# Two half-width matmul tiles, and seven products for eight, in the third layer of a four-layer graph kernel

## The chip, the cores and the metric

The kernel runs on one core of one Trainium2 chip. The metric is the device time of one execution in microseconds (us). Before the change it is 2273.68 us, the median of three runs (2272.29 to 2274.11).

## What is computed

There are 32 independent graphs (batches) of 512 nodes with 128 features, each with a dense weighted 512 x 512 adjacency matrix, everything in fp32. Four graph layers follow each other; each normalizes its input, applies a graph network and adds the result to its input. What matters here is the third of them ("stage three"), which is itself a network of four sublayers over the same adjacency matrix:

```python
def _layer(nodes, adj, ws, bs, wd, bd, wn, bn, wu, bu):
    src = nodes @ ws + bs
    src_agg = jnp.einsum('bjv,bij->biv', src, _l2norm(adj, 2))
    dst = nodes @ wd + bd
    dst_agg = jnp.einsum('bjv,bji->biv', dst, _l2norm(adj, 1))
    self_rep = nodes @ wn + bn
    upd = jnp.concatenate([src_agg, self_rep, dst_agg], axis=2)
    return jnp.tanh(upd @ wu + bu)
...
for i in range(NUM_LAYERS):
    if i < half:
        stashed.append(fpass)
    elif i == half:
        fpass = jnp.concatenate([fpass, stashed[NUM_LAYERS - i - 1]], axis=2)
    else:
        fpass = jnp.concatenate([fpass, stashed[NUM_LAYERS - i], stashed[NUM_LAYERS - i - 1]], axis=2)
    fpass = _layer(fpass, adj, *params[i])
```

So each sublayer multiplies projected features with the matrix (aggregation over the rows) and with its transpose, and adds a term of the node itself. Sublayers 2 and 3 also take `f1`, the output of sublayer 0, and sublayer 3 takes `f0`, the input of all.

## The kernel before

All work of a batch is listed as operations of an engine with an estimated time, what they read and what they write (`Plan.op`). `Plan.order` then plays all 32 batches through at once: on each engine the ready operation with the earliest due time goes first (due times lie `PERIOD` = 37 us a batch apart), and an operation waits in the plan until its buffers are free. The result is a fixed instruction order for each engine, with several batches interleaved on TensorE (PE). The buffers are places in a few pools: `s2` (a 128 x 512 tile, 36 of them), `s4` (twice as much, 5), `s8` (a whole matrix, 10) and 8 PSUM banks. Where the plan leaves PE idle for more than 0.7 us, `kept_warm` puts in products of the identity (`ps_idle`).

In stage three, `w_sb` holds weights into which the update matrix `wu` has been multiplied at the start, so that aggregation, node term and update fall together. Per batch:

- `a` and `aT`, the matrix and its transpose as four chunks of 128 x 512, are scaled in place by the inverse norms (L1096, DVE).
- Sublayers 0 and 2 (loop at L1107): `paired_rows` makes `sd`, both projections with bias (4 matmuls of 256 columns, L791 adds the bias); a node term of 512 columns and eight aggregation matmuls of 512 columns go into one PSUM bank (`ps_agg`), and tanh on ScalarE (ACT) ends the sublayer.
- Sublayer 1 with `fifteen` (L871 and on): eight aggregation matmuls of the turned features `f1r`, then 15 products of 256 columns, which give the terms of `f1` and of its two aggregates in sublayers 1, 2 and 3 at once (nine matrix products of two halves each would be 18). The sums before and after them are on DVE (L908).
- Sublayer 3 with `seven`: its projections of two inputs as seven products for eight, 14 matmuls of 128 columns, with DVE sums (L813); then two node terms and eight aggregation matmuls.

`mm` (L353) emits nearly all matmuls, `product` those of `fifteen` (L914), of `seven` (L835) and of the last layer's gates (L516). The stationary operand has 128 columns in all of them. `at_ends` (the first two batches and the last) turns matrices by PE transposes (`ps_t`, L733, L753, L876); the others turn them by DMA. GpSimd (POOL) does the negative half powers of the normalizations (L688, L1077) and nothing wide.

## Time and profile before

| | |
|---|---|
| median of three runs | 2273.68 us |
| the profiled execution's own time | 2275.95 us |
| its span | 2274.2 us |
| matmul operations, in two records each but for transposes, which have one | 3844 |
| DVE busy, mean step of a 128x512 operation | 1607.0 us, 687 ns |
| GpSimd's powers of 128x4 and 128x8 | 1186 ns and 1857 ns |

The span is from the first to the last instruction of the program; the execution's own time lies 1.75 us above it. "Busy" is time in which an engine had any instruction under way. For PE the lengths of matmuls overlap, so the pace is read from one start to the next.

### The profile page before, as it was taken

Reading aid. Unit: us, or ns where it says so; the run is one execution under the profiler, and the core shown is the slowest. Engines: PE = TensorE matmul, PEld = TensorE weight load, DVE = VectorE, ACT = ScalarE, POOL = GpSimd, SP = SyncE. Lnnn points to the kernel's source line nnn. Section 1 sums busy time; section 2 is a strip of 40 time slices with the busy share of each in tenths; the row PEclk is TensorE's granted clock in tenths of the full one; section 3 lists DMA queues with packets and bytes.
Section 4 is the critical chain, followed back from the end, with each engine's and each line's share of the span. In section 5 each row is a group of like instructions: output and inputs, shape, how many; then the busy total and the mean of one; then the engine's idle time right before and its main releaser. Section 6 shows DMA issues by size and latency. Waiting matters only on the chain.

```text
span 2274.2 us, 25755 instructions
## 1 busy us (share of the span) xinstructions
PE 2263.3 (100%) x7608; PEld 1311.8 (58%) x7608; DVE 1607.0 (71%) x4346; ACT 1101.4 (48%) x2563; POOL 216.6 (10%) x203
## 2 busy tenths in 40 slices
PE   9999999999999999999999999999999999999999
PEld 6555565555565555555555655555555556555556
DVE  6756676767777777767777777777677777776655
ACT  7643554544445544455544455445555444552422
POOL 2100100100100100001001001000010010010000
PEclk9999999999999999999999999999999999999999
DMA  8032333444333443334443334443344333333212
GB/s 295 29 105 77 111 99 117 139 128 127 119 105 121 130 130 120 107 117 135 132 123 121 104 120 130 130 120 108 115 136 134 122 117 106 121 99 91 79 42 65
DMA packets 199052, 263.03 MB, mean 116 GB/s; under 512 B 25984, under 2 KB 130688, under 8 KB 198912
## 3 DMA queue, kind: packets, MB, share of 16 engines
q1 hardware_dynamic: 198624, 261.26, 37.6%
q8 instruction: 60, 0.98, 0.2%
q14 instruction: 80, 0.66, 0.1%
q10 hardware_dynamic: 288, 0.13, 0.0%
HBM read 199.18 MB, written 62.13 MB: 115 GB/s over the span
## 4 chain that ended last, share of the span: by engine, by line
PE 95%; DMA 2%; DVE 2%; ACT 0%; issue 0%; SPq 0%; POOL 0%; ACTq 0%; DVEq 0%; POOLq 0%
PE ps_agg L353 61%; PE ps_fifteen L914 9%; PE ps_sd L353 7%; PE ps_seven L835 4%; PE ps_seven L516 4%; PE ps_upd L353 3%; PE ps_gate L353 3%; PE ps_lin L353 1%; PE ps_msg L353 1%; PE ps_node L353 1%; DMA last<-turn_last 0%; DMA turned<-turn_turned 0%; DMA bounce<-invT 0%; DMA r_sb<-in_brow 0%; DMA turn_turned<-blk 0%; DMA rows<-bounce 0%
## 5 line engine op out<-in xcount | busy, mean ns | idle before, releaser
L353 PE MATMUL ps_agg<-a,sd 128*128 128x512 f32 x768 | 385.3, 593 | 0.0
L353 PE MATMUL ps_agg<-aT,sd 128*128 128x512 f32 x768 | 380.5, 593 | 0.4 <-DVE sd L791 0.2
L688 POOL TENSOR_TENSOR sc<-v,neg_half 128x4 f32<-128x4 f32 (+1 forms) x127 | 150.6, 1186 | 1710.5 <-DVE v L649 1603.5
L353 PEld LDWEIGHTS ps_agg<-aT,sd 128*128 128x128 f32 x768 | 136.6, 191 | 86.4 <-issue 77.5
L700 ACT ACTIVATE h<-xr,nb,sc 128x128 f32<-128x128 f32 x384 | 157.9, 482 | 49.1 <-DVE nb L696 49.1
L353 PEld LDWEIGHTS ps_agg<-a,sd 128*128 128x128 f32 x768 | 137.0, 191 | 62.0 <-issue 53.8
L353 PE MATMUL ps_sd<-w_sb,f 128*128 128x256 f32 x512 | 145.6, 380 | 0.9 <-ACT f L1112 0.9
L353 PEld LDWEIGHTS ps_sd<-w_sb,f 128*128 128x128 f32 x512 | 94.4, 190 | 77.6 <-issue 61.7
L1136 ACT ACTIVATE f<-c,cf_sb 128x512 f32<-128x512 f32 x64 | 46.2, 722 | 179.8 <-DVE c L1135 179.8
L353 PE MATMUL ps_agg<-f,w_sb 128*128 128x512 f32 x256 | 130.9, 593 | 0.1
L353 PE MATMUL ps_agg<-aT,f1r 128*128 128x512 f32 x256 | 130.7, 592 | 0.0
L353 PE MATMUL ps_agg<-a,f1r 128*128 128x512 f32 x256 | 130.7, 592 | 0.0
L353 PE MATMUL ps_agg<-aT,h 128*128 128x512 f32 (+2 forms) x260 | 128.7, 583 | 0.6 <-ACT h L673 0.6
L353 PE MATMUL ps_agg<-a,rep 128*128 128x512 f32 x256 | 125.5, 592 | 0.0
L353 PE MATMUL ps_agg<-aT,rep 128*128 128x512 f32 x256 | 121.6, 595 | 2.0 <-DVE rep L1049 1.8
L353 PE MATMUL ps_agg<-aT,msg 128*128 128x512 f32 (+1 forms) x264 | 116.7, 579 | 0.0
L791 DVE TENSOR_TENSOR sd<-ps_sd,rf_sb 128x512 f32<-128x512 f32 x128 | 87.9, 687 | 32.3 <-PE ps_sd L353 31.9
L1096 DVE TENSOR_TENSOR a<-a,rows 128x512 f32<-128x512 f32 x128 | 87.2, 687 | 16.7 <-PE ps_agg L353 16.1
L709 DVE STREAM_TRANSPOSE blk<-h 128x512 f32<-128x512 f32 x87 | 61.4, 706 | 51.4 <-ACT h L700 51.2
L1077 POOL TENSOR_TENSOR inv<-stat,neg_half 128x8 f32<-128x8 f32 x32 | 59.4, 1857 | 308.8 <-DVE stat L1076 287.9
L1096 DVE TENSOR_TENSOR aT<-aT,rows 128x512 f32<-128x512 f32 x128 | 86.4, 684 | 2.0 <-PE ps_agg L353 1.9
L1136 ACT ACTIVATE f<-ps_agg,cf_sb 128x512 f32<-128x512 f32 x32 | 22.0, 687 | 131.8 <-PE ps_agg L353 131.8
(229 smaller groups left out, 4424.6 us busy)
## 6 DMA issues: line engine op xcount, KB each, us to landing
aT<-in_adjt SPq DMA_DIRECT2D x124, 512.0 KB, 3.9
turn_turned<-blk SPq DMA_DIRECT2D x696, 64.0 KB, 1.8
turned<-turn_turned SPq DMA_DIRECT2D x174, 256.0 KB, 2.7
a<-in_adj SPq DMA_DIRECT2D x62, 512.0 KB, 7.5
rows<-bounce SPq DMA_DIRECT2D x32, 512.0 KB, 3.7
shares<-bounce SPq DMA_DIRECT2D x32, 512.0 KB, 4.4
x<-in_x SPq DMA_DIRECT2D x32, 256.0 KB, 2.7
out<-xr SPq DMA_DIRECT2D x31, 256.0 KB, 3.1
```

Source lines behind the costliest of these rows:

```text
L353: op("PE", t_mm(n), lambda: nc.tensor.matmul(out_of(ps.ap()), lhs(), rhs(), start=start, stop=stop), reads, [ps], later=later)
L516: op("PE", t_mm(H), lambda: nc.tensor.matmul(o[0](), weight(), data[0](), start=first, stop=True, skip_group_check=True), [data[1], wbuf], ...
L688: op("POOL", t_pow(n), lambda: nc.gpsimd.tensor_tensor(inv.ap()[:, :n], v8.ap()[:, :n], neg_half[:, :n], op=ALU.pow), [v8, NH], [(inv, {0})])
L700: op("ACT", t_act(D, 2), lambda c=c: nc.scalar.activation(h.ap()[:, c, :], xin.ap()[:, c, :], AF.Relu, bias=nb.ap()[:, c:c + 1], scale=inv ...
L709: op("DVE", t_tt(N), lambda: nc.vector.transpose(blk.ap().rearrange("p b (c r) -> p c b r", c=NC), m.ap().rearrange("p c (b s) -> p c b s" ...
L791: op("DVE", t_tt(N), lambda ps=ps, h=h: nc.vector.tensor_add(sd.ap()[:, 2 * h:2 * h + 2, :], ps.ap().rearrange("p (j v) -> p j v", j=2), a ...
L835: op("PE", t_mm(D), lambda j=j: nc.tensor.matmul(ps.ap()[:, k * H + j * D:k * H + (j + 1) * D], lhs()[:, j * P:(j + 1) * P], rhs(), start= ...
L914: op("PE", t_mm(H), lambda: nc.tensor.matmul(o[0](), weight(), data[0](), start=first, stop=True, skip_group_check=True), [data[1], wbuf], ...
L1077: roots = op("POOL", t_pow(2 * NC) + 0.4, lambda: nc.gpsimd.tensor_tensor(inv.ap()[:, :2 * NC], stat.ap(), neg_half, op=ALU.pow), [stat, N ...
L1096: op("DVE", t_tt(N), lambda m=m, c=c, s=s: nc.vector.tensor_mul(m.ap()[:, c, :], m.ap()[:, c, :], rows.ap()[:, s, :]), [(m, {c}), rows], [ ...
L1136: end = op("ACT", t_act(N, 1), lambda to=to, i=i, f_new=f_new: nc.scalar.activation(f_new.ap(), to.ap(), AF.Tanh, bias=cf_sb[:, i:i + 1]), ...
```

## The change

- Every matmul is now two: `by_halves` takes columns 0 to 63 and 64 to 127 of the stationary operand, one after the other, into the lower and upper 64 partitions of the output. This holds for the idle products too. PE transposes become such products with the identity (`turn_on_pe`).
- The aggregations of all four sublayers take seven products for eight: the matrix is seen as 2 x 2 blocks (even and odd chunk of a pair, left and right half of the columns), the features likewise (even and odd chunk, lower and upper 64). `made_of` prepares three combinations of blocks for each of `a` and `aT` on GpSimd (and replaces one block in place); `left_sums` makes four for the features on DVE. `side_by_side` emits two products with different operands, one for each half of the array.
- `features` replaces the node term, the aggregation and tanh of sublayers 0, 2 and 3. `lo` and `hi` list the products of the two halves in order; the sums of the seven products lie on DVE and one copy on ACT; tanh is taken in three parts.
- `fifteen` goes. `edges` makes the two aggregates of `f1` by the seven products, `second` adds the three terms of sublayer 1 as plain products, and the same three sources are node terms of `features` in sublayers 2 and 3.
- `seven` goes: `paired_rows` projects both inputs of sublayer 3 (8 matmuls of 256 columns).
- The pools become `s2` 29, `s4` 6, `s6` 4 (the combinations), `s8` 8; `PERIOD` becomes 41 us.

```diff
--- before.py
+++ after.py
@@ -22,17 +22,17 @@
 LN_EPS = 1e-5
 NORM_EPS = 1e-12
 L2_CHUNKS = (1, 1, 2, 3)
-PERIOD = 37.0
+PERIOD = 41.0
 ENDING = -3.5
...
-GATES = 5 * D
-FIFTEEN = GATES + 4 * D
-T_COLS = FIFTEEN + 6 * D
-LAYER_OF = (2, 3, 1)
+GATES = 0
+NODE = GATES + 4 * D
+T_COLS = NODE + 10 * (D // 2)
+HALVES = slice(0, P // 2), slice(P // 2, P)
...
@@ -296,7 +296,7 @@
-    plan = Plan(sb, psum, {"bank": 8, "s2": 36, "s4": 5, "s8": 10}, {"bank": 0, "s2": 4, "s4": 0, "s8": 0})
+    plan = Plan(sb, psum, {"bank": 8, "s2": 29, "s4": 6, "s6": 4, "s8": 8}, {"bank": 0, "s2": 3, "s4": 0, "s6": 0, "s8": 0})
...
@@ -349,21 +349,25 @@
+    def by_halves(to, weight, data, start, stop):
+        for c in HALVES:
+            nc.tensor.matmul(to[c], weight[:, c], data, start=start, stop=stop, skip_group_check=True)
+
     def mm(ps, out_of, lhs, rhs, n, start, stop, reads, later=0.0):
-        op("PE", t_mm(n), lambda: nc.tensor.matmul(out_of(ps.ap()), lhs(), rhs(), start=start, stop=stop),
-           reads, [ps], later=later)
-
-    LAST = [W_L2[3][0] + (2 * k + o) * D for k in (2, 0) for o in range(2)]
+        op("PE", t_mm(n), lambda: by_halves(out_of(ps.ap()), lhs(), rhs(), start, stop), reads, [ps], later=later)
+
+    def turn_on_pe(ps, part, columns, reads):
+        op("PE", t_mm(P), lambda: by_halves(ps.ap()[:, part * P:(part + 1) * P], columns(), ident, True, True), reads + [ID], [(ps, {part})])
+
     BOTH = [c + k * D for c in (W_L3_HH, W_L3_IH) for k in range(2)]
 
-    def third(k, o):
-
-        i = LAYER_OF[o]
+    def of_first(i, k):
+
         n = 0 if i == 1 else 1
         return W_L2[i][1] + n * D if k == 2 else W_L2[i][0] + (2 * n + k) * D
 
-    def t15(k):
-        return t_sb[:, FIFTEEN + k * D:FIFTEEN + (k + 1) * D]
+    NODES = {0: [W_L2[0][1]], 1: [], **{i: [W_L2[i][1]] + [W_L2[i][1] + 2 * D] * (i == 3) + [of_first(i, k) for k in (2, 0, 1)] for i in (2, 3)}}
+    NODE_AT = {(i, n): len(NODES[0]) * (i > 0) + len(NODES[2]) * (i > 2) + n for i in NODES for n in range(len(NODES[i]))}
 
     def setup():
 
...
+        for (i, n), k in NODE_AT.items():
+            op("DVE", t_tt(D // 2), lambda k=k, c=NODES[i][n]: nc.vector.tensor_sub(
+                t_sb[:, NODE + k * (D // 2):NODE + (k + 1) * (D // 2)], w_sb[:, c:c + D // 2], w_sb[:, c + D // 2:c + D]),
+               [(W2F, {i})], [(TS, {NODE + k})])
-        def weigh(dst, x, y, how):
...
@@ -513,7 +487,7 @@
             def product(o, data, weight, wbuf, first):
-                op("PE", t_mm(H), lambda: nc.tensor.matmul(o[0](), weight(), data[0](), start=first, stop=True, skip_group_check=True), [data[1], wbuf], [o[1]])
+                op("PE", t_mm(H), lambda: by_halves(o[0](), weight(), data[0](), first, True), [data[1], wbuf], [o[1]])
@@ -730,8 +704,7 @@
             if at_ends:
                 ps = plan.bank("t")
                 for c in range(NC):
-                    op("PE", 0.109, lambda c=c: nc.tensor.transpose(ps.ap()[:, c * P:(c + 1) * P], m.ap()[:, c * P:(c + 1) * P], ident),
-                       [m, ID], [(ps, {c})])
+                    turn_on_pe(ps, c, lambda c=c: m.ap()[:, c * P:(c + 1) * P], [m])
...
@@ -786,95 +758,206 @@
...
-        def seven(x1, x2, dst, part, behind):
...
+        H, Q = N // 2, D // 2
+
+        def region(m, rows, at):
+            return lambda: m.ap()[HALVES[rows], at * H:(at + 1) * H]
+
+        def two(m, k, j):
+            return lambda: m.ap().rearrange("p (q k) n -> p q k n", k=2)[:, :, k, j * H:(j + 1) * H]
+
+        def summed(engine, eng, us, o, x, y, sign, reads, writes):
+            op(engine, us, lambda: eng.tensor_tensor(o(), x(), y(), op=ALU.subtract if sign < 0 else ALU.add), reads, writes)
+
+        def added(o, x, y, reads, writes, n=H):
+            summed("DVE", nc.vector, t_tt(n), o, x, y, 1, reads, writes)
+
+        def made_of(m):
+
+            tm, even, odd = buf("s6", (P, 2, 3, H), "made"), {0, 2}, {1, 3}
 
             def t(k):
+                return lambda: tm.ap()[:, :, k, :]
+
+            for o, x, y, reads, writes in (
+                    (t(1), two(m, 1, 1), two(m, 0, 1), [m], [(tm, {1})]),
+                    (two(m, 0, 1), two(m, 0, 1), two(m, 0, 0), [(m, even)], [(m, even)]),
+                    (t(0), two(m, 1, 1), two(m, 0, 1), [m], [(tm, {0})]),
+                    (t(2), two(m, 1, 0), t(0), [(m, odd), (tm, {0})], [(tm, {2})])):
+                summed("POOL", nc.gpsimd, 1.6, o, x, y, -1, reads, writes)
+            return tm
+
...
+        def left_sums(n, part, src, st, place):
+
+            for k, x, y, sign, reads in (
+                    (0, part(1, 0), part(1, 1), 1, []), (1, place(0), part(0, 0), -1, [0]),
+                    (2, part(0, 0), part(1, 0), -1, []), (3, part(0, 1), place(1), -1, [1])):
+                summed("DVE", nc.vector, t_tt(n), place(k), x, y, sign, [src] + [(st, {j}) for j in reads], [(st, {k})])
+
+        def side_by_side(lo, hi, begun):
+            for pair in zip(lo, hi, strict=True):
...
+                def emit(emits=emits):
+                    for to, lhs, rhs, start in emits:
+                        nc.tensor.matmul(to(), lhs(), rhs(), start=start, stop=True, skip_group_check=True)
+
+                op("PE", t_mm(H), emit, reads, writes)
+
+        def features(i, sd, nodes, made, f_new):
+
+            st = buf("s4", (P, 4, NC, Q), "st")
+            left_sums(H, lambda h, k: lambda: sd.ap().rearrange("p (q k) (o h f) -> p q k o h f", k=2, o=2, h=2)[:, :, k, :, h, :],
+                      sd, st, lambda k: lambda: st.ap()[:, k].rearrange("p (q o) f -> p q o f", q=2))
+
+            def products(to, k, qs):
+                made_here = []
+                for q in qs:
...
+                return made_here
+
+            def node(to, h, j):
+                made_here = []
+                for n, (data, reads) in enumerate(nodes):
+                    k, c = NODE_AT[i, n], NODES[i][n] + h * Q
+                    made_here.append((*to, (lambda k=k: t_sb[:, NODE + k * Q:NODE + (k + 1) * Q]) if h == 2 else (lambda c=c: w_sb[:, c:c + Q]),
+                                      lambda data=data: data()[:, j * H:(j + 1) * H], [reads(j), (TS, {NODE + k}) if h == 2 else (W2F, {i})]))
+                return made_here
+
+            ab, cd = plan.bank("ab"), plan.bank("cd")
+            A, Bh, C, Dh = ((region(x, r, 0), (x, {r})) for x in (ab, cd) for r in range(2))
+            q4, q2 = range(4), range(2)
+            lo = products(A, 1, q4) + products(C, 5, q4) + node(C, 1, 1) + products(A, 2, q4) + node(A, 0, 0) + products(C, 3, q2)
+            hi = products(Bh, 6, q4) + node(Dh, 2, 1) + products(Dh, 3, (2, 3)) + products(Bh, 7, q4)
+            second = len(hi)
+            hi += products(Bh, 4, q4) + node(Bh, 1, 0)
+            begun, p1, to = set(), buf("s2", name="p1"), buf("s2", name="to")
...
+            side_by_side(lo[:4], hi[:4], begun)
+            copy(p1_lo, A)
+            add(d, p1_lo, Bh)
+            side_by_side(lo[4:second], hi[4:second], begun)
+            add(e, p1_lo, Bh)
+            add(quarter[1, 1], e, C)
+            side_by_side(lo[second:], hi[second:], begun)
+            add(d, d, C)
+            add(quarter[0, 1], d, Dh)
+            add(quarter[1, 0], p1_lo, Bh)
+
+            def tanh(rows, cols, src, reads, n):
+                op("ACT", t_act(n, 1), lambda: nc.scalar.activation(f_new.ap()[rows, cols], src(), AF.Tanh, bias=cf_sb[rows, i:i + 1]), reads + [(CF, {i})], [f_new])
+
+            tanh(HALVES[0], slice(0, H), A[0], [A[1]], H)
+            tanh(HALVES[1], slice(0, N), lambda: to.ap()[HALVES[1], :], [(to, {2, 3})], N)
+            tanh(HALVES[0], slice(H, N), quarter[0, 1][0], [quarter[0, 1][1]], H)
+            return plan.ops[-1]
+
+        def edges(f1r, made, ge):
+
...
+            left_sums(P, part, f1r, st, lambda k: lambda: st.ap()[:, k])
+            banks = [plan.bank(n) for n in ("a2", "b2", "c2")]
...
+            products(0, 1)
+            op("ACT", t_act(H), lambda: nc.scalar.copy(p(), whole(0)()), [banks[0]], [p1])
+            products(1, 6)
+            added(d, p, whole(1), [p1, banks[1]], [(de, {0})])
+            products(2, 5)
+            products(0, 2)
...
+            products(1, 7)
+            added(e, p, whole(1), [p1, banks[1]], [(de, {1})])
+            out(1, 1, de, 1, {1}, 2)
+            products(1, 4)
+            out(1, 0, p1, 0, {0}, 1)
+            products(2, 3)
+            out(0, 1, de, 0, {0}, 2)
+
-        def fifteen(f1, shares):
...
+        def second(f1, shares, made):
...
+            edges(f1r, made, ge)
+
+            sources = [(f1.ap, lambda j: f1)] + [((lambda k=k: ge.ap()[:, k, :]), (lambda j, k=k: (ge, {k + 2 * j}))) for k in range(2)]
+            ps, f2p = plan.bank("second"), buf("s2", name="f2p")
+            for n, (k, (data, _)) in enumerate(zip((2, 0, 1), sources, strict=True)):
+                mm(ps, lambda t: t, lambda k=k: wt(of_first(1, k)), data, N, n == 0, n == 2, [(ge, {k, k + 2}) if n else f1, (W2F, {1})])
...
@@ -1101,40 +1105,25 @@
         f0 = transposed(h2, "f0")
         f = f0
 
...
+        made = [made_of(m) for m in (aT, a)]
         for i, (wsd, wn) in enumerate(W_L2):
             f_new = buf("s2", name=f"f{i + 1}")
             if i == 1:
                 share([second_features])
-                to, *later = fifteen(f, shares)
+                to, sources = second(f, shares, made)
                 op("ACT", t_act(N, 1), lambda to=to, f_new=f_new: nc.scalar.activation(f_new.ap(), to.ap(), AF.Tanh, bias=cf_sb[:, 1:2]),
                    [to, (CF, {1})], [f_new])
                 f = f_new
                 continue
+            nodes = [(f.ap, lambda j, f=f: f)]
             if i == 3:
-                sd = buf("s4", (P, NC, 2 * D), "sd")
-                seven(f0, f, *of_halves(sd), [third_started])
+                sd = paired_rows([f0, f], [wsd + 4 * D, wsd], (W2F, {i}), rf_sb, RF, ROW_OF[i] * 2 * D)
+                nodes.append((f0.ap, lambda j: f0))
             else:
-                sd = paired_rows([f], wsd, (W2F, {i}), rf_sb, RF, ROW_OF[i] * 2 * D)
-            ps = plan.bank("agg")
-            linear_t(ps, [wn, wn + 2 * D] if i == 3 else [wn], [f, f0] if i == 3 else [f], (W2F, {i}), stop=False)
-
-            order = [(0, 0), (1, 1), (1, 0), (0, 1)] if i == 3 else [(0, 0), (1, 0), (0, 1), (1, 1)]
-            for h, o in order:
-                m, lo = ((aT, 0), (a, D))[o]
-                for c in (2 * h, 2 * h + 1):
-                    mm(ps, lambda t: t, lambda c=c, lo=lo, sd=sd: sd.ap()[:, c, lo:lo + D], lambda c=c, m=m: m.ap()[:, c, :], N,
-                       False, (h, o) == order[-1] and c % 2 == 1, [(sd, {2 * c + o}), (m, {c})])
-            to = ps
-            if i == 2:
-                third_started = plan.ops[-1]
+                sd = paired_rows([f], [wsd], (W2F, {i}), rf_sb, RF, ROW_OF[i] * 2 * D)
             if i > 1:
-                to = later[i - 2]
-                op("DVE", t_tt(N), lambda ps=ps, to=to: nc.vector.tensor_add(to.ap(), ps.ap(), to.ap()), [ps, to], [to])
-            end = op("ACT", t_act(N, 1), lambda to=to, i=i, f_new=f_new: nc.scalar.activation(f_new.ap(), to.ap(), AF.Tanh, bias=cf_sb[:, i:i + 1]),
-                     [to, (CF, {i})], [f_new])
+                nodes += sources
+            end = features(i, sd, nodes, made, f_new)
...
@@ -1167,7 +1156,7 @@
     def idle_products(slot, n):
         ps = psum.tile([P, N], F32, name="ps_idle", tag=f"bank_{slot}", bufs=1)
         for _ in range(n):
-            nc.tensor.matmul(ps[:, :P], ident, ident, start=True, stop=True)
+            by_halves(ps[:, :P], ident, ident, True, True)
```

## The prediction

> **What bounds the kernel now.** I read the page first: the engine totals, the clock row and the chain that ended last.
>
> ```profile
> span 2274.2 us, 25755 instructions
> PE 2263.3 (100%) x7608; PEld 1311.8 (58%) x7608; DVE 1607.0 (71%) x4346; ACT 1101.4 (48%) x2563; POOL 216.6 (10%) x203
> PEclk9999999999999999999999999999999999999999
> PE 95%; DMA 2%; DVE 2%; ACT 0%; issue 0%; SPq 0%; POOL 0%; ACTq 0%; DVEq 0%; POOLq 0%
> ```
>
> TensorE is occupied throughout at full clock, and the chain is 95% PE. "Busy" alone proves little for pipelined matmuls, so next comes the view of waits for PE, which shows that nothing holds it up (under 8 us in all), and the chain in order of time, whose 10.30 us pieces return once a batch:
>
> ```profile
> PE ps_agg L353 <- DVE rep L1049: 1.8, 3, 1.2
> PE ps_idle L1170 <- POOL ident masks.py:199: 1.4, 1, 1.4
> PE ps_sd L353 <- ACT f L1112: 0.9, 1, 0.9
> ...
> 335.49 10.30 PE ps_agg L353 x24
> 404.87 10.30 PE ps_agg L353 x24
> 474.24 10.30 PE ps_agg L353 x24
> ```
>
> So one batch costs 69.38 us, and 32 of them 2220 us of the 2274.2; the rest is the ramp at both ends. Last, the timeline of PE, for the pace of one matmul (columns: start, length, and two records for each fp32 matmul):
>
> ```profile
> 1000.37 0.59 PE L353 MATMUL ps_sd<-w_sb,f 128*128 128x256 f32 x2
> 1000.80 0.59 PE L914 MATMUL ps_fifteen<-xy,w_sb 128*128 128x256 f32 x2
> 1001.24 0.59 PE L914 MATMUL ps_fifteen<-col,t_sb 128*128 128x256 f32 x2
> ...
> 1015.50 1.02 PE L353 MATMUL ps_agg<-a,sd 128*128 128x512 f32 x2
> 1016.36 1.02 PE L353 MATMUL ps_agg<-aT,sd 128*128 128x512 f32 x2
> 1017.22 1.02 PE L353 MATMUL ps_agg<-a,sd 128*128 128x512 f32 x2
> 1018.08 0.38 PE L835 MATMUL ps_seven<-t_sb,f 128*128 128x128 f32 x2
> ...
> 21.57 0.75 PEld L353 LDWEIGHTS ps_foldb<-c_sb,raw 128*128 128x128 f32 x6
> 22.24 0.53 PEld L353 LDWEIGHTS ps_foldb<-raw,c_sb 128*128 128x128 f32 x4
> ```
>
> Starts, not lengths, count, since lengths overlap. 512 columns: 0.86 (I use 0.859); 256: 0.43 (0.432); 128: 0.22 (0.222, as at 1018.08 to 1018.30). The last two lines are six weight loads of 128 columns in 0.67 us, 0.112 each, in front of matmuls with one moving column: that is the pace of the load path, and twice 0.112 is what a 128-column matmul costs. Check with the plan's instruction counts (1847 of 512 columns, 1101 of 256, 808 of 128, 80 transposes): 1586.6 + 475.6 + 179.4 + 80 x 0.111 + 2 for small ones = 2252.5 us. The kernel is its column count.
>
> **What the skill says.** "TensorEngine Tiling (Array Packing)", Key Properties: tiles of the array load weights and multiply independently, and a change of tiling mode drains TensorE; no run here shows a tile yet. "TensorE: Matmul & The Clock Gate", Part 3: packed matmuls start in program order, about 4 ns apart, and their weight loads are pulled ahead. The trace of before shows loads only one matmul ahead[...]. "SBUF — State Buffer", Who interferes with whom: a DVE operation with two SBUF inputs and a GpSimd operation that reads SBUF exclude each other. The trace shows none of this for small powers: GpSimd's 1.64 us one at 1027.93 did not hold up DVE's two-input one at 1028.76 (0.69 us).
>
> **The change, part by part.**
>
> *Columns of one middle batch.* Before: 58 matmuls of 512, 34 of 256, 22 of 128 = 49.8 + 14.7 + 4.9 = 69.4 us, which is the period seen. After, in pairs of halves, one pair counted as one full matmul: `edges` 14 x 256 for the eight aggregations of layer 1; `second` 3 x 512 for part of the fifteen; `features` 16, 22 and 24 x 256 for layers 0, 2 and 3 (14 for the aggregations and 2 for each node term: one, four, five of them, the three sources among them as plain terms); `sd` of layer 3 as 8 x 256 in place of `seven`. That makes 25 of 512, 103 of 256, 8 of 128 = 21.5 + 44.5 + 1.8 = 67.8 us. In units of 256 columns: the aggregations of four layers save 2 each, 8 in all; the plain terms give back 3 (6 + 12 for 15), `seven` one (8 for 7). Net 4 units less a little for more short matmuls: 1.6 us a batch, 52 us in all.
>
> *At the ends.* 80 transposes become plain matmuls: + 80 x 0.111 = 8.9. The order of instructions has 110 idle pairs where before had 63 products: 47 x 0.222 = + 10.4; they fill gaps, so the gaps at the ends grow by that much. None stand in the middle.
>
> *Sum over the whole program* by the after counts (791, 3309 and 487 pairs of 512, 256, 128): 679.5 + 1429.5 + 108.1 + 2 = 2219.1, so -33.4 us if a pair costs just what a full matmul does.
>
> *What a pair costs* is not in this trace. Below nothing: each half still streams its columns twice, so it can't undercut 2 x 0.216; I take 0 as the lower end. Upper ends: starts in order with 4 ns at each of two switches, +8 ns (an estimate from the Part 3 figure), 4595 pairs x 0.008 = +37 us; loads that don't pass a queued matmul, below; no overlap, twice the time. With 128 columns there are four loads of 64 for two of 128: 0.112 is 0.107 of columns at 1.2 per ns (an estimate from the section LDWEIGHTS of the same page) and 5 ns besides, so +10 ns on 487 pairs, +5 us. I take +2 ns a pair, +9 us, and +5: the start-to-start of 216 for 213 of streaming leaves only 2 to 3 ns of issue to be paid at a switch.
>
> *DVE, ACT.* DVE loses 960 operations of 256 and 192 of 512 and gains 1216, 64 and 128 of 128: at 0.333, 0.605 and about 0.2 a step (timeline) -436 + 470 = +34 us, to 72%. ACT: -166 + 232 = +66 us, to 51%. Both lie under PE's 97%; cost nothing while the order keeps several batches going. If that cover goes, every late sum holds the in-order PE.
>
> *GpSimd.* 256 subtractions of 512 elements, new. Nearest row: none; the "GPSIMD Engine Reference", 3.1, gives 2.6 cycles an element, an estimate of 1.1 us; the plan's own entry is 1.6. So 282 to 410 us, 10% to 22 to 28%: no bound. They queue with the powers of the layer norms, each up to 1.6 us later, and if they shut DVE out, up to 256 x 1.1 us of DVE delay, DVE to 84%. Behind it stand the sums that PE waits for; before had 8 us of such waits. I take +4 us, range 0 to 60.
>
> *Buffers.* s8 goes from 10 to 8, s2 from 36 to 29: fewer batches overlap; it is in the order already (no idle products mid-way), so 0. SP issues the same 1382 instructions.
>
> Total: -33.4 + 9 + 5 + 4 = -15.4 on the profiled execution's 2275.95 us (1.75 around the span) = 2260.5. The median shown lies 2.3 under that execution: 2258; I say 2257.
>
> **Rivals.** *(1) The pair costs too much in issue.* From +5.3 ns a pair ((33.4 - 5 - 4) us over 4595) the gain is gone. At +8 and the other small terms: 2273.7 - 33.4 + 37 + 9 = 2286. For: gaps per matmul are paid twice as often, eight TensorE instructions for four. Against: the one-column matmuls show starts far below 0.216. Slower. *(2) Loads wait behind a queued matmul.* The second half's first load stands in program order after the first half's second pass. If it starts only with that pass, each switch costs the lead of a load, some 30 ns (among the one-column matmuls a load starts at 21.68 and its matmul at 21.71), 60 a pair: 4595 x 0.06 = +276, 2520 us. Slower. *(3) Halves don't overlap at all:* 2219 twice, about 4470; the change then doesn't do what it says. *(4) GpSimd and DVE shut each other out* and PE waits: the 60 us above, 2257 + 45 = 2300. *(5) Pairs hide what a full matmul pays between passes:* 3 ns a pass, 6 a pair, -27: about 2230.
>
> **Numbers.** Side by side, small extra: 0.50, at 2240 to 2268. (5) 0.04. Costs that meet the gain within 0.2% (4.5 us, about what a measurement tells from none): 0.08. (1) 0.15, (4) 0.09, (2) 0.11, (3) 0.03. Faster 0.53, same 0.08, slower 0.39. The range, 2236 to 2330, leaves out (2), (3) and part of (5); the likeliest case alone spans 2240 to 2268.
>
> **What would show it.** Right: PE at 98% or more, no PE wait over 10 us, 64-column records of the first and second half that overlap, a batch period of 68 to 68.5 us, DVE near 1640. Rival (1): the same, but 0.44 from pair to pair at 256 columns; (2): 0.49; (3): 0.86. Rival (4): waits of PE for DVE sums, and DVE operations of 256 elements that last over 1 us beside GpSimd's. The weakest step is the pair's price: 5 ns decide the sign.

## The result, and the profile after

The changed kernel takes 2359.81 us (median of 4 runs, 2357.24 to 2363.44) against 2272.98 us of the kernel before beside it: a ratio of 1.0384, with a 95% interval of 1.0366 to 1.0402. It is slower by 87 us, where 16 us less were forecast. The page of the profile after, engine totals, clock and the summary of the chain that ended last:

```profile
span 2357.9 us, 48190 instructions
...
PE 2275.6 (97%) x18380; PEld 1403.2 (60%) x18380; DVE 1810.0 (77%) x4592; ACT 1183.5 (50%) x2723; POOL 562.4 (24%) x459
...
PEclk9999999999999999999999999999999999999999
...
PE 61%; DVE 22%; DMA 7%; issue 3%; ACT 3%; POOL 2%; SPq 1%; DVEq 0%; ACTq 0%; POOLq 0%
```

The chain was 95% PE; it is 61% now, and DVE holds 22% of it. PE is no longer the only thing that counts. The clock row rounds: the mean granted clock is 0.996. Inside the span there are five stretches at half clock, one of 6.8 us near the start and four of 3.4 us later. Each goes with an idle time of PE of 2.4 us or more (other idle times of that length have none), and in the four a pass of 256 columns takes 0.427 us, where it otherwise takes 0.216. That costs about 7 us (an estimate: half of 4 x 3.4 us). The kernel before has none before its last 2 us. The waits of PE (in all, how often, the longest, us), which came to under 8 us before:

```profile
PE ps_msg L354 <- ACT hT L730: 39.2, 27, 2.6
PE ps_second L354 <- DVE ge L777: 20.2, 28, 0.9
PE ps_idle L354 <- DVE xr L708: 6.0, 1, 6.0
```

The first two come once a batch. Now the pace of the pairs, in the timeline of PE (start, length, and four records for each pair of halves):

```profile
1016.70 1.03 PE L354 MATMUL ps_second<-f,w_sb 128*64 128x512 f32 x4
1017.56 1.03 PE L354 MATMUL ps_agg<-aT,h 128*64 128x512 f32 x4
...
1019.28 1.94 PE L354 MATMUL ps_second<-ge,w_sb 128*64 128x512 f32 x8 [0.70 <-DVE ge L777]
...
1023.60 2.36 PE L354 MATMUL ps_sd<-w_sb,f 128*64 128x256 f32 x20
1025.76 1.07 PE L354 MATMUL ps_lin<-w_sb,agg 128*64 128x128 f32 x16
...
1029.12 0.44 PE L354 MATMUL ps_msg<-w_sb,hT 128*64 128x128 f32 x4 [1.86 <-ACT hT L730]
1029.39 0.38 PE L823 MATMUL ps_cd<-aT,st 128*64 128x256 f32 x1
1029.40 0.38 PE L823 MATMUL ps_cd<-f,t_sb 128*64 128x256 f32 x1
```

A 512-column pair takes 0.86 us to the next start (1016.70 to 1017.56), five of 256 take 2.16 (1023.60 to 1025.76, 0.432 each), four of 128 take 0.87 (1025.76 to 1026.63, 0.218 each). These are the prices of full matmuls before: 0.859, 0.432, 0.222. The last two lines are the two halves of one pair of `features`, started within 0.01 us. So the pairs cost what the sum gave them. What is lost is lost in the brackets: 0.70 us for a DVE sum and 1.86 us for the turned features `hT`. Where those come from is seen on DVE and GpSimd in the same stretch; the groups of instructions first (out<-in, shapes, count, then busy us and mean ns):

```profile
L1100 DVE TENSOR_TENSOR a<-a,rows 128x512 f32<-128x512 f32 x128 | 134.6, 1070 | 0.9 <-PE ps_agg L354 0.9
L1100 DVE TENSOR_TENSOR aT<-aT,rows 128x512 f32<-128x512 f32 x128 | 86.5, 680 | 2.5 <-DMA rows<-bounce 1.4 <-PE ps_agg L354 1.0
L670 DVE SCALAR_TENSOR_TENSOR nb<-mv,sc 128x4 f32<-128x4 f32 x127 | 51.5, 406 | 44.8 <-POOL sc L662 43.8
L777 POOL TENSOR_TENSOR made<-aT 128x512 f32<-128x512 f32 x64 | 93.2, 1457 | 948.0 <-DVE aT L1100 835.6 <-PE ps_ab L823 46.4 <-DMA turn_turned<-blk 30.8
L777 POOL TENSOR_TENSOR made<-a,made 128x512 f32<-128x512 f32 x32 | 40.7, 1273 | 2.2
```

`a<-a,rows` and `aT<-aT,rows` are the same operation on the same shape, at 1070 and 680 ns; a tiny `nb` of four elements takes 406 ns on average (161 before). The timeline shows which ones:

```profile
1009.17 2.97 DVE L1100 TENSOR_TENSOR a<-a,rows 128x512 f32<-128x512 f32 x2
...
1015.30 0.17 DVE L623 TENSOR_SCALAR v<-mv 128x4 f32<-128x4 f32 x1
...
1016.59 1.22 DVE L670 SCALAR_TENSOR_TENSOR nb<-mv,sc 128x4 f32<-128x4 f32 x1 [0.40 <-POOL sc L662]
1017.84 0.85 DVE L777 TENSOR_TENSOR ge<-p,ps_b 64x256 f32<-64x256 f32 x2
...
1013.85 1.27 POOL L777 TENSOR_TENSOR made<-aT 128x512 f32<-128x512 f32 x1
1015.55 1.01 POOL L662 TENSOR_TENSOR sc<-v,neg_half 128x4 f32<-128x4 f32 x1 [0.43 <-DVE v L623]
1016.53 1.27 POOL L777 TENSOR_TENSOR a<-a 128x512 f32<-128x512 f32 x1
```

Two `a<-a,rows` took 2.97 us together beside GpSimd's combinations. `nb`, started 0.06 us after a combination at 1016.53, ends at 1017.81, when that combination ends. Behind it in DVE's queue stand the `ge` sums, for which PE waits at 1019.28, and through `nb`, the rectified `h`, the transposing transfer and `hT` the wait at 1029.12. Of the DVE operations that overlap a combination, 88 `a<-a,rows` have a median of 1292 ns, against 680 for the 40 that don't, and 30 `nb` have 1224 against 163. In all, DVE is busy for 92 us more than in a run below in which GpSimd reads nothing (1810.0 against 1718.3). Operations with a PSUM input (`ge`, `de`, and the few `p`, `to` and `sd` that overlap one) and the transposes show no difference.

### The profile page after: what moved, and what is told of

The parts are those of the page before. It is cut to its first block, busy times and chain, and to the rows that moved or that the text cites. A ratio compares the mean times of both kernels' runs of the same rounds, so it can differ in the third digit from the quotient of the medians.

```text
span 2357.9 us, 48190 instructions
## 1 busy us (share of the span) xinstructions
PE 2275.6 (97%) x18380; PEld 1403.2 (60%) x18380; DVE 1810.0 (77%) x4592; ACT 1183.5 (50%) x2723; POOL 562.4 (24%) x459
## 4 chain that ended last, share of the span: by engine, by line
PE 61%; DVE 22%; DMA 7%; issue 3%; ACT 3%; POOL 2%; SPq 1%; DVEq 0%; ACTq 0%; POOLq 0%
PE ps_ab L823 20%; PE ps_cd L823 13%; PE ps_agg L354 8%; PE ps_sd L354 7%; DMA turned<-turn_turned 4%; DVE a L1100 4%; PE ps_seven L354 4%; DVE aT L1100 3%; DVE ge L777 3%; PE ps_gate L354 2%; PE ps_second L354 2%; PE ps_msg L354 1%; DVE st L777 1%; DMA turn_turned<-blk 1%; POOL sc L662 1%
## 5 line engine op out<-in xcount | busy, mean ns | idle before, releaser
L823 PE MATMUL ps_ab<-made,st 128*64 128x256 f32 x1536 | 412.2, 382 | 1.6 <-DVE st L777 1.6
L354 PE MATMUL ps_sd<-w_sb,f 128*64 128x256 f32 x2048 | 265.8, 379 | 0.0
L823 PE MATMUL ps_ab<-aT,sd 128*64 128x256 f32 x768 | 226.5, 383 | 0.0
L823 PE MATMUL ps_cd<-aT,st 128*64 128x256 f32 x768 | 223.7, 381 | 1.4 <-DVE st L777 1.4
L823 PE MATMUL ps_ab<-a,sd 128*64 128x256 f32 x768 | 225.0, 381 | 0.0
L823 PE MATMUL ps_cd<-a,st 128*64 128x256 f32 x768 | 221.4, 383 | 0.0
L823 PEld LDWEIGHTS ps_ab<-made,st 128*64 128x64 f32 x1536 | 209.1, 138 | 12.5 <-DVE st L777 2.5
L354 PEld LDWEIGHTS ps_sd<-w_sb,f 128*64 128x64 f32 x2048 | 164.8, 137 | 68.6 <-issue 16.4
L823 PE MATMUL ps_ab<-made,sd 128*64 128x256 f32 x768 | 198.7, 381 | 0.0
L823 PE MATMUL ps_ab<-f,w_sb 128*64 128x256 f32 x768 | 190.1, 379 | 0.0
L1100 DVE TENSOR_TENSOR a<-a,rows 128x512 f32<-128x512 f32 x128 | 134.6, 1070 | 0.9 <-PE ps_agg L354 0.9
```

What stands on the lines that cost most here:

```text
L354: nc.tensor.matmul(to[c], weight[:, c], data, start=start, stop=stop, skip_group_check=True)
L823: nc.tensor.matmul(to(), lhs(), rhs(), start=start, stop=True, skip_group_check=True)
L1100: op("DVE", t_tt(N), lambda m=m, c=c, s=s: nc.vector.tensor_mul(m.ap()[:, c, :], m.ap()[:, c, :], rows.ap()[:, s, :]), [(m, {c}), rows], [ ...
```

## The experiments

The theories, as the expectations name them. X: GpSimd's wide operations read SBUF and hold DVE's operations with two SBUF inputs; DVE is late and PE waits. X2: the combinations stand in GpSimd's queue in front of the powers that the normalizations need. Y: fewer buffers and longer chains leave too little cover. Y2: the plan runs each result just in time, so that any lateness shows. Z: pairs cost more than full matmuls.

**The pairs alone.** The kernel before, with every matmul by halves and transposes as products; order and algorithm are those of before.

```diff
-        op("PE", t_mm(n), lambda: nc.tensor.matmul(out_of(ps.ap()), lhs(), rhs(), start=start, stop=stop),
+        op("PE", t_mm(n), lambda: by_halves(out_of(ps.ap()), lhs(), rhs(), start, stop), reads, [ps], later=later)
```

> The kernel before with every matmul as two half-width ones and its transposes as products with the identity, nothing else; the plan is untouched. If a pair costs what a full matmul does, only the 80 transposes and the ends add: 2273 + 9 = 2282 us, at most 2285. With 2 ns a pair (as the prediction took) 2290; with 8 ns (rival 1) 2313; with 60 ns (rival 2) over 2500. The trace of the changed kernel lets me expect 2276 to 2284.

Measured: 2277.84 us, ratio 1.0027 (1.0016 to 1.0037), +5.7 us, less than the 8.9 that the transposes alone were put at. No wait of PE comes to 2 us in all. Theory Z falls.

**The smaller pools alone**, in the kernel before:

```diff
-    plan = Plan(sb, psum, {"bank": 8, "s2": 36, "s4": 5, "s8": 10}, {"bank": 0, "s2": 4, "s4": 0, "s8": 0})
+    plan = Plan(sb, psum, {"bank": 8, "s2": 29, "s4": 5, "s8": 8}, {"bank": 0, "s2": 3, "s4": 0, "s8": 0})
```

> The kernel before with the pools of the changed one (s2 29 instead of 36 with 3 kept, s8 8 instead of 10; s4 stays 5). Theory Y says that fewer batches in flight make PE wait: over 2300 us. Theory X: the pools matter little, under 2290 us; two more short gaps in the plan's order cost some 2 us.

Measured: 2273.56 us, ratio 1.0007 (0.9998 to 1.0015). The pools cost the kernel before nothing. That they cost the changed one nothing isn't shown by it.

**The combinations on DVE instead of GpSimd:**

```diff
-                summed("POOL", nc.gpsimd, 1.6, o, x, y, -1, reads, writes)
+                summed("DVE", nc.vector, t_tt(N), o, x, y, -1, reads, writes)
```

> The changed kernel with the 256 subtractions that prepare the matrix (made_of) on DVE instead of GpSimd, at the plan's own price for a 512-element DVE operation. Theory X (GpSimd's wide operations that read SBUF shut out DVE's operations with two SBUF inputs, DVE falls behind the plan, PE waits): a<-a,rows falls from 1070 to about 685 ns, nb from 406 to about 165 ns, PE's idle time from 82 us to under 35 us, the span to 2260 to 2290 us although DVE has 155 us more work. Theory Y (the chains are longer and the buffers fewer, so the cover is thin whatever shuts out what): PE still waits for hT and ge, 2330 us or more, worse if DVE becomes the bound. Theory Z (the pairs cost more than full matmuls): about 2350 us.

Measured: 2335.12 us, ratio 1.0275 (1.026 to 1.029). `a<-a,rows` is back at 681 ns and `nb` at 160, as the hold demands, but the time is far above the 2260 to 2290 of theory X: DVE has 256 operations more (1839.6 us busy, 79%). The waits of PE in this run:

```profile
PE ps_cd L823 <- DVE st L777: 22.7, 27, 1.7
PE ps_second L354 <- DVE ge L777: 20.7, 27, 1.5
```

The work costs DVE as much as the hold did, at other places. Moving it doesn't separate X from Y; taking it away does.

**GpSimd writes only.** Three memsets for each combination, whose values are left out: the same queue place and about the same length (some 1.6 to 1.9 us), but nothing is read.

```diff
-                summed("POOL", nc.gpsimd, 1.6, o, x, y, -1, reads, writes)
+                op("POOL", 1.6, lambda o=o: [nc.gpsimd.memset(o(), 0.01) for _ in range(3)], reads, writes)
```

> The changed kernel in the same instruction order on every other engine, with each wide GpSimd subtraction replaced by three memsets of the same output, which read nothing. The combinations of the matrix blocks are left out. GpSimd is still occupied for about a microsecond each time. Theory X: DVE's a<-a,rows at 685 ns, nb at 165 ns, PE idle under 35 us, time 2260 to 2285 us. Theory X2 (it is GpSimd's queue, with the powers of the layer norms behind the wide operations, that makes hT late): DVE's durations fall as in X, but PE still waits for hT by some 40 us, about 2320 us. Theory Y: 2340 us or more.

Measured: 2291.81 us, ratio 1.009 (1.0073 to 1.0107), with GpSimd busier than in the changed kernel (610.9 us). This is a little above the range of theory X. PE's wait for `ge` is all but gone (0.4 us), and that for `hT` is halved, where theory X2 had some 40 us left:

```profile
PE ps_msg L354 <- ACT hT L730: 19.6, 27, 2.4
```

So 68 of the 117 us above the column sum (2275.95 - 33.4 = 2242.6) come with what GpSimd's combinations read and wait for; the half clock is in them, since this run has no such stretch. An operation that reads nothing also waits for less, so this takes away two things at once. The next four runs look at each apart.

**A late DVE without any hold.** In the run above and in the kernel before, scratch products of 256 elements (`held`) stand in DVE's queue: one before each `a<-a,rows`, three before the `nb` of the last layer, 74 us in all (the hold adds 92).

```diff
+    def held(n):
+        nc.vector.tensor_mul(scratch[:, :n], w_sb[:, :n], w_sb[:, :n])
...
-                op("DVE", t_tt(N), lambda m=m, c=c, s=s: nc.vector.tensor_mul(m.ap()[:, c, :], m.ap()[:, c, :], rows.ap()[:, s, :]),
+                op("DVE", t_tt(N), lambda m=m, c=c, s=s: (held(2 * P) if s else None, nc.vector.tensor_mul(m.ap()[:, c, :], m.ap()[:, c, :], rows.ap()[:, s, :])),
...
-        h3, _ = normed(x3, "h")
+        h3, _ = normed(x3, "h", late=True)
```

> The memset variant (GpSimd reads nothing, the combinations are left out) with DVE held up by hand where GpSimd held it up in the changed kernel: one scratch product of 256 elements before each a<-a,rows (128 of them, 0.33 us each) and three before the nb of the last layer's norm (31, 1.0 us), 74 us of DVE that the plan does not know. Theory X in its strict form (the late DVE operations alone make the loss, GpSimd itself does nothing else): 2335 to 2360 us with waits for hT and ge back. If something else of GpSimd's subtractions costs the time (their queue, their longer chain): under 2315 us.

> The kernel before with the same 74 us of unplanned DVE operations at the same places. Theory Y2 (the changed kernel's plan runs TensorE just in time, that of before had slack, so that the same lateness costs it little): under 2290 us. If any plan suffers alike: 2315 us or more.

Measured: the changed order 2322.44 us, 30.6 more than without, between the two ranges expected; the kernel before 2284.01 us, ratio 1.0048 (1.003 to 1.0065), 11.6 more, as expected. The same delay costs the changed order 2.6 times as much. But 37 of the 68 us are still missing.

**GpSimd's wait for its data, without the long reads.** As the run of memsets, but each combination first subtracts two columns of its inputs, so that it can't start before they are there; in the second kernel with the scratch products too.

```diff
-                op("POOL", 1.6, lambda o=o: [nc.gpsimd.memset(o(), 0.01) for _ in range(3)], reads, writes)
+                op("POOL", 1.6, lambda o=o, x=x, y=y: (nc.gpsimd.tensor_tensor(o()[:, :, :2], x()[:, :, :2], y()[:, :, :2], op=ALU.subtract), [nc.gpsimd.memset(o()[:, :, 2:], 0.01) for _ in range(3)]), reads, writes)
```

> Left out, as in e2: the combinations that GpSimd makes (their values are wrong, so the third stage's output is too). Against e2, GpSimd's eight wide operations a batch now wait for the data that the real ones wait for: each first subtracts two columns of the two inputs, then fills the rest with three memsets. e2 gave 2291.8 us, the changed kernel 2359.8; the vector engine's lateness alone (e7) gave back 31 of the 68. Theory X (the hold on the vector engine is the whole matter): the two-column subtractions are short, the vector engine is not held, so 2288 to 2298, with a<-a,rows near 0.69 us. Rival W (the other half of the 68 us is GpSimd's wait for its own inputs, which the memsets of e2 did not have): 2315 to 2335 with a<-a,rows still near 0.69 us.

> e9 and e7 together (combinations left out as in both): GpSimd waits for its data, and the vector engine has the 74 us of hand-placed scratch products. If lateness of the vector engine and GpSimd's data wait together are what the changed kernel pays, 2345 to 2365, the changed kernel's 2359.8. If e7's 2322 stays (2318 to 2332), neither explains the rest, and the places of the holds do or something not yet named.

Measured: 2328.64 us (1.0238, 1.0215 to 1.0261), 36.8 more than the memsets alone, with `a<-a,rows` at 685 ns; and 2360.84 us (1.0383, 1.0358 to 1.0408) for both, which is the changed kernel's time. The first lies where rival W had it, the second where both delays together were expected. The timeline shows what the 36.8 us are in this run. With memsets alone:

```profile
1051.13 0.17 DVE L623 TENSOR_SCALAR v<-mv 128x4 f32<-128x4 f32 x1
...
1052.93 0.12 DVE L670 SCALAR_TENSOR_TENSOR nb<-mv,sc 128x4 f32<-128x4 f32 x1
...
1051.38 1.01 POOL L662 TENSOR_TENSOR sc<-v,neg_half 128x4 f32<-128x4 f32 x1 [2.73 <-DVE v L623]
```

and once they wait for `aT` and `a`:

```profile
1070.95 0.31 DVE L623 TENSOR_SCALAR v<-mv 128x4 f32<-128x4 f32 x1
...
1074.01 0.16 DVE L670 SCALAR_TENSOR_TENSOR nb<-mv,sc 128x4 f32<-128x4 f32 x1 [1.18 <-POOL sc L662]
...
1069.55 1.69 POOL L795 MEMSET made<- 128x508 f32 x3
1071.19 0.20 POOL L795 TENSOR_TENSOR made<-aT 128x4 f32<-128x4 f32 x1
1071.33 1.68 POOL L795 MEMSET made<- 128x508 f32 x3
1072.96 1.01 POOL L662 TENSOR_TENSOR sc<-v,neg_half 128x4 f32<-128x4 f32 x1
```

The power `sc` has its place between the fourth and the fifth combination. Its input is there at 1071.26; it starts at 1072.96, when the fourth is through, 1.70 us late, and `nb` with it. In the first run the memsets had been done before and the power starts at once. (It lasts 1.01 us; the 1186 ns in the table ahead are a mean over two shapes.) So each of the two delays costs time by itself, and both end in the same `nb`. Its end, counted from the batch's first `aT<-aT,rows` on DVE, and the period of that operation, medians over 26 batches, in us:

```
                                   nb ends   period
memsets                              13.06    69.51
memsets after their data             14.36    70.63
memsets, DVE late                    14.50    70.41
both                                 15.50    71.49
changed kernel                       15.07    71.37
combinations behind nb (below)       13.06    72.30
memsets, DVE lighter (below)         13.06    69.63
```

In the second to fifth rows, each microsecond by which `nb` is later than in the first goes with 0.6 to 0.9 us a batch. No run makes this `nb` alone late.

In the changed kernel itself the power does not wait for the queue. GpSimd is free at 1015.12, the late `v` ends at 1015.47, and the power waits for it (`<-DVE v L623` above). By the medians of the 26 batches `v` ends 1.42 us later than in the run of memsets, behind the held `a<-a,rows`, and 0.36 us after GpSimd is free; then `nb` is held itself, for 1.1 us. So the hold (X) accounts for all of the 2.01 us by which `nb` is late there. The queue (X2) is what would come next: with the same combinations and a punctual `v` the power would start up to 0.98 us late (12.37 instead of 11.39 us on the scale of the table, an estimate). The run that waits for its data makes the queue longer than it is, since a stand-in takes 1.9 us (0.20 + 1.69) and a combination 1.27 to 1.66. So 31 and 37 are not the parts of the 68 us, and that their sum meets the changed kernel's time within 1 us is in part luck: `nb` ends 0.43 us later in the run with both. How the 68 us divide stays open.

**A plan that knows of it.** Two tries to let the plan allow for the delays: DVE's times raised by 8% and `a<-a,rows` by 0.45 us in the changed kernel (`PERIOD` 41), and DVE's times raised by 8% in the kernel with the combinations on DVE (`PERIOD` 43).

```diff
+        us *= 1.08 if engine == "DVE" else 1.0
...
-                op("DVE", t_tt(N), lambda m=m, c=c, s=s: nc.vector.tensor_mul(m.ap()[:, c, :], m.ap()[:, c, :], rows.ap()[:, s, :]),
+                op("DVE", t_tt(N) + 0.45 * s, lambda m=m, c=c, s=s: nc.vector.tensor_mul(m.ap()[:, c, :], m.ap()[:, c, :], rows.ap()[:, s, :]),
```

> The changed kernel, GpSimd as it is, with a plan that knows better: DVE's operations 8% dearer and each a<-a,rows 0.45 us dearer. No other edit. Theory X with a plan that was blind: PE's waits fall by half or more and the time lies at 2280 to 2310 us. If the shut-outs hurt wherever they fall: 2340 us or more.

> The combinations on DVE (no GpSimd operation wide), DVE's operations 8% dearer in the plan, due times 43 us apart instead of 41. Theory Y2 (what remains of the loss without shut-outs is a plan without slack on DVE): PE idle under 50 us, 2262 to 2290 us, perhaps under the kernel before. If DVE's 155 us more work are themselves the bound: 2320 us or more, as before the repricing (2335).

Measured: 2340.74 us (1.0301, 1.0286 to 1.0317), 19 less than the changed kernel; and 2342.59 us (1.0308, 1.0291 to 1.0325), 7 more than without the raise. The better ends of both expectations failed. In the first, the plan itself leaves more gaps (197 idle pairs in place of 110), the waits for `hT` are gone and others have come:

```profile
PE ps_sd L355 <- ACT f L1115: 16.8, 27, 1.3
PE ps_ab L824 <- ACT f L887: 14.6, 31, 1.6
```

**The combinations moved away from the powers.** The changed kernel whole; in 27 batches six combinations stand behind the `nb` that was late and two behind the next one. In the first kernel a small subtraction on GpSimd that reads `nb` holds them back; in the second they follow the powers directly.

```diff
+            one, two = norms[norms.index(pool[k + 4]):][:2]
+            for power, part in ((one, eight[:6]), (two, eight[6:])):
+                nb = min((n for n in power.next if n.engine == "DVE"), key=where.get)
+                put[nb] = part
...
+            if o in put:
+                nb = next(x for x in o.bufs if x.kind == "nb")
+                tell = plan.op("POOL", 0.2, lambda nb=nb: nc.gpsimd.tensor_tensor(spare, nb.ap(), nb.ap(), op=ALU.subtract))
+                out.append(tell)
+                out += put[o]
```

> The changed kernel whole, with one thing moved in 27 of the 32 batches: GpSimd's eight combinations, which surround the power of the third stage's neighbouring normalisation, stand six behind that normalisation's nb and two behind the nb of the next normalisation (a small subtraction on GpSimd that reads nb holds them back). Every other queue keeps its order. The first reader of a combination comes 30 us after the power in the plan, so they still arrive in time. If what the changed kernel pays is that GpSimd's combinations hold the vector engine's a<-a,rows and nb, and stand in front of the power (theories X and X2 together, 31 and 37 of the 68 us by e7 and e9), the time goes to 2290 to 2315, a<-a,rows to near 0.69 us and nb to 0.2 us or less. If the loss is in the new order of the matmuls whatever GpSimd does (rival Y), 2340 to 2360.

> As e11, without the small subtraction: the six combinations stand right behind the power and may hold the nb that reads it; the two behind the next power likewise. a<-a,rows is free of the hold and the power no longer stands behind combinations; only nb is held, up to 1.3 us in each of 27 batches and in two places. Theory: each microsecond of a late nb costs up to a microsecond a batch, so e11 plus 20 to 40 us, 2315 to 2345. If nb's lateness is covered elsewhere, e11's time within 8 us.

Measured: 2379.55 us (1.046, 1.0445 to 1.0474) and 2371.24 us (1.0424, 1.041 to 1.0438): both slower than the changed kernel. Both expectations failed, though `nb` is back at 13.06 in the first and at 13.66 in the second. The groups of DVE in the first of them say why:

```profile
L777 DVE TENSOR_TENSOR st<-st,sd 128x256 f32<-128x256 f32 x96 | 70.7, 736 | 0.1
L980 DVE SCALAR_TENSOR_TENSOR f2p<-shares,b_sb,f2p 128x512 f32<-128x512 f32 x32 | 47.1, 1473 | 1.0
L487 DVE TENSOR_TENSOR s<-hT 128x256 f32<-128x256 f32 x31 | 42.1, 1358 | 2.6 <-ACT hT L730 2.5
...
L670 DVE SCALAR_TENSOR_TENSOR nb<-mv,sc 128x4 f32<-128x4 f32 x127 | 23.2, 183 | 37.1 <-POOL sc L662 35.9
```

`nb` and `a<-a,rows` are free, and the hold has gone to other operations with two SBUF inputs: 736, 1473 and 1358 ns where the changed kernel has 432, 751 and 419, and `xr<-turned,xr` 1001 for 702. DVE is busy for 1836.3 us, 26 more than in the changed kernel, and PE waits for `p`, `st` and transfers, each in place of part of the wait for `hT`. By the count at the end of this section, one half of the array works alone for some 25 us more than in the changed kernel. In the second kernel 57 `nb` and 58 `st<-sd` run beside a combination, with medians of 1219 and 1485 ns. The expectation looked only at where the hold had been, not at what DVE runs in the new place.

**What remains without GpSimd's reads.** The run of memsets still stands 49 us above the column sum, and its period is 69.51 us where 67.8 was forecast, which over 31 batches is 53. To see whether DVE's lateness is in that too, the 128 products `a<-a,rows` were left out, with all orders kept, there and in the kernel before.

```diff
-                op("DVE", t_tt(N), lambda m=m, c=c, s=s: nc.vector.tensor_mul(m.ap()[:, c, :], m.ap()[:, c, :], rows.ap()[:, s, :]),
+                op("DVE", t_tt(N), lambda m=m, c=c, s=s: None if s else nc.vector.tensor_mul(m.ap()[:, c, :], m.ap()[:, c, :], rows.ap()[:, s, :]),
```

> Left out: GpSimd's combinations (memsets, as in e2) and the vector engine's 128 products a<-a,rows (87 us of its work; the scaling of a), with every order unchanged. e2 stands at 2291.8 us, some 48 above what its matmuls' columns come to (2243). If the vector engine's own lateness is still what the matmuls wait for in e2, a lighter vector engine gives 2255 to 2275. If the 48 us are in the chains of matmul, scalar engine, transposing transfer and matmul, or in the pairs of halves themselves, 2284 to 2292.

> The kernel before with the same 128 products a<-a,rows left out. It waits for nothing long (matmuls 98 to 99% busy), and 74 us more of vector engine cost it 11.6; 87 us less should give it nothing: 2266 to 2273. More than 8 us of gain would say that it too stands at the vector engine.

Measured: 2290.84 us (1.0074, 1.0056 to 1.0092), no gain over 2291.81; and 2272.78 us (0.9993, 0.9984 to 1.0002). A lighter DVE at this place doesn't help: `nb` ends at 13.06 as before, since in DVE's order it stands behind a transpose that waits for ACT (`blk<-y`, 0.99 us in the run of memsets). The waits of PE are as they were:

```profile
PE ps_msg L354 <- ACT hT L730: 21.1, 26, 2.0
```

What the 49 us are made of can be counted from the starts of the matmul records, with 427, 213 and 107 ns of array time for a pass of 512, 256 and 128 columns. For the time in which two halves, one, or none are under way, in us:

```
                     both    one   none   both + one/2
pairs alone        2218.9   37.8   13.4         2237.8
memsets            2149.3   86.0   50.0         2192.3
changed kernel     2147.3   90.1  116.2         2192.4
```

The change does take the work away: 45 us of array time against the kernel with pairs alone (37 against the 2229.3 of full matmuls). In the run of memsets 37 us of it go into time in which nothing runs (of its 50 us, 25.5 lie before `ps_msg`, where `hT` is late), and 24 into time in which one half of the array has work and the other none. In the changed kernel the idle time is 66 us more still; about 10 of it is the half clock, which this count takes for idle. Whether a different order could win the 49 us was not tried beyond the two raised plans; it stays open.

## Why the prediction was wrong, step by step

Forecast and measured time lie 103 us apart. On top of the column sum of 2242.6 us the forecast put 9 and 5 us for pairs and 4 for GpSimd, and took off 3.6 to come to the median and a round number. The runs show 68 us that come with GpSimd's combinations, where 4 were allowed, and 49 that stay without their reads, where only the 14 for pairs were allowed, which cost nothing.

- *Columns of one batch and of the program.* Right: -33.4 us forecast, -37.0 counted in array time.
- *What a pair costs.* Taken at +9 us, and +5 for pairs of 128; measured nothing (0.432 and 0.218 us against 0.432 and 0.222). With it rivals (1), (2), (3) fall: in the run of pairs alone the loads of both halves start 2 ns after a pass has begun and the pace stays that of full matmuls. The step called the weakest was sound, if 14 us too dear. The Trainium skill, "TensorE: Matmul & The Clock Gate", Part 3, on which the upper end was built, has packed matmuls start about 4 ns apart; the starts here lie 4 to 36 ns apart, but that offset is not paid again at each pair. The same part of the page lets a load overlap a matmul under way only in another group of rows, which the prediction left out; two halves of the columns share their rows, and the loads ran ahead all the same.
- *GpSimd.* This step failed. It named the hold and the powers in its queue "each up to 1.6 us later", and took "+4 us, range 0 to 60" for both. Measured: 68 us. The pieces were near: 346 us of added GpSimd time (282 to 410 forecast), a subtraction of 1.27 us where nothing holds it (1.1 to 1.6), a power 1.4 us late (behind `v`, not behind GpSimd's queue as forecast), 92 us of held DVE. What was mis-sized is the cover. DVE at 72% was read as a queue with slack; but one late `nb` stands in front of the sums and of the transfer that PE takes next, once in every batch, and a microsecond of it went with 0.6 to 0.9 us of time in the runs above. Some 7 us of the 68 are the half clock after PE's longer waits, for which the forecast had no term. The Trainium skill, "SBUF — State Buffer", Who interferes with whom, gave the mechanism that the trace of after confirms: two SBUF inputs against a GpSimd read exclude each other for the whole instruction (`nb` at 1016.59 ends with the combination beside it), and operations with one SBUF and one PSUM input are not touched (`ge`, 418 ns). The trace of before could show neither, as it has no wide GpSimd operation.
- *DVE and ACT.* "Cost nothing while the order keeps several batches going" failed too: with pairs at no cost, the 49 us that stay without GpSimd's reads belong to this term, which was put at nothing. That DVE and ACT alone make them isn't shown. DVE's own work grew by 111 us, not 34 (1718.3 us in the run of memsets, without the hold): the forecast used the step of operations that follow each other, 0.333 us (and 0.605 for 512 elements, whose mean length is the 687 ns of the table ahead), while the groups of the new sums have a mean of 0.42 and part of them stand alone; how much of the 77 us that explains stays open. ACT grew by 82 us, not 66. And the order keeps less in hand: 74 us of DVE delay cost it 30.6 us, and the kernel before 11.6.
- *Buffers.* "So 0" holds for the kernel before with the smaller pools; what they do to the changed order was not isolated.
- *The period.* 68 to 68.5 us was to show it right; it is 71.37, and 69.51 without the reads, the 69.4 of before. Of the gain of 1.6 us a batch nothing arrives even without GpSimd.
- *Rival (4)* named the cause and its sign: waits of PE for DVE sums, DVE operations over 1 us beside GpSimd's. It was priced at 45 us with 60 as its end, and given 0.09. It also looked at 256-element sums, most of which have a PSUM input and are free; the ones held were others.

## What to carry to other kernels

When wide work is put on an idle engine, list what its instructions exclude and what stands behind them in its queue, find the one small operation among these that another engine's next work hangs on, and price each delay there at a large part of its length a batch (0.6 to 0.9 here), whatever the busy shares say. Fewer products saved no time here because the order had no other work ready while PE waited for the sums and transfers they add; an in-order PE at 100% with no waits is a reason to ask how late each of its inputs could be, not a sign that there is cover. To take a hold away, look first at what would be held in the new place.

## What the runs showed of the hardware

- Two tiles of 64 columns sustain the pace of a full array in fp32: 0.858, 0.432 and 0.218 us for a pair of 512, 256 and 128 columns, with twice the instructions, and 2277.84 against 2272.09 us for a whole kernel in pairs.
- A DVE operation of four elements with two SBUF inputs lasts as long as the GpSimd operation beside it: `nb`, 163 ns alone, 1224 ns as a median beside a combination.
- The hold works both ways: GpSimd's subtractions of 512 elements take 1273 ns where DVE leaves them alone and 1444 to 1582 in the groups that run beside `a<-a,rows`.
- GpSimd's memsets do not hold DVE's operations with two SBUF inputs: with 610.9 us of GpSimd time beside it, `a<-a,rows` stays at 684 ns. They do hold a small operation with one input: six `v` of 128x4 that overlap memsets have a median of 420 ns, against 170 for those beside no GpSimd work.
- GpSimd's powers of 128x4 and 128x8 show no such hold: in the kernel before, 29 `a<-a,rows` beside one have a median of 693 ns, against 685 for the others.
- In fp32 a pass of 256 columns takes 0.427 us in the stretches granted at half clock and 0.216 at full. In the changed kernel these stretches last 3.4 us, begin within 1 us of the end of an idle time of PE of 2.5 to 2.8 us, and two idle times of 2.4 and 2.5 us went without one.
